# Second layer's value projection: two sets of half products with a written VectorE order in place of half products for five batches and direct matmuls for two

## The chip, the cores and the metric

The kernel runs on one core of one Trainium2 chip. The metric is the device time of one execution in microseconds (us); the time before the change is the median of three runs.

## The reference

Two layers of cross attention on x of 8 batches x 100 rows x 1024 against one context of 8 x 1444 x 512, all float32. The first layer takes a softmax over the context, the second over the query rows; the second ends in a layer norm.

```python
Q = x @ Wq + bq;  K = ctx @ Wk + bk;  V = ctx @ Wv + bv
w = softmax(Q K^T * 1024**-0.5, axis=-1)
x = x + (w @ V) @ Wo + bo                     # layer 0
q = x @ Wq + bq;  k = ctx @ Wk + bk;  v = ctx @ Wv + bv
w = softmax(q k^T * 1024**-0.5, axis=1)       # layer 1: over the rows
x = x + w @ v
out = (x - mean) * rsqrt(var + 1e-6) * gamma + beta
```

## The kernel before, in words

Keys and values are never made. `weight_products` folds Wq with Wk and Wv with Wo, `queries` multiplies x by the folded matrix, and `scores` multiplies the result by the context (transposed, `cT`, 4 units of 128 features). The weighted context A = ctx^T w (512 x 100 for a batch) is made first by `weighted_rows` (48 matmuls, line 513), and only then multiplied by the value matrix. x is held transposed in `xT` (8 blocks of 128 features x 800 columns, 100 for each batch), and the value projections add into it (`add_to_queries`, line 608).

**The loop of the second layer** (lines 864 to 887) takes the batches in turn. In `alternated` one matmul of batch b's A is followed by one score matmul of batch b + 2 (44 of them for the 48 of A); in batch 5 (`doubled`) it is followed by two, so that batch 7's scores are done halfway. Batches 6 and 7 have no scores ahead. When scores are complete, ScalarE copies them out of four PSUM banks (line 554), and `softmax1` (line 643) makes weights of them: 16 transposes of 32 x 384 on VectorE (line 589), then for each of three groups of rows a maximum (line 656), four exponentials on ScalarE (line 658), a reciprocal and a scaling on VectorE (lines 661, 662), and at last seven operations on GpSimd that sum the weights of a batch (`weight_sums`). `weight_totals` (line 682) transposes these sums of two batches on TensorE; they multiply the value bias later.

**The value projection of the second layer** is done in three sets. Batches 0 to 4 (columns 0 to 499) go after batch 5, in `project1_halves` (line 700): a 2 x 2 block product with seven half products in place of eight (`seven_products`, line 172), each of 8 matmuls of width 250, with sums of blocks on VectorE for the right side (`right_sums`) and on GpSimd, ahead of time, for the left (`project1_sums`). The right sums overwrite blocks of A1T and so have to follow products that read them. Batches 5 and 6 go after batch 6, in `project1` (line 712), as 32 plain matmuls of width 200. Batch 7 goes last, in `project_last` (line 777).

**The finish** of a batch (line 770): 8 transposes of its `xT` columns on TensorE (line 741), two passes on VectorE that add the bias term (line 745), two of statistics (line 751), and `normalise`: a power on GpSimd (line 759), a pass on VectorE (line 760), a scaling on ScalarE (line 762), an addition of beta on GpSimd (line 763) and the output DMA from GpSimd's queue (line 764). Batches 0, 1, 2 are finished under batch 6's A, 3 and 4 in whole blocks around the projection of 5 and 6, and 5 and 6 under batch 7's A. Batch 7's own finish closes the kernel: `untransposed`, `project_last`, and two output DMAs from SP and ScalarE.

**What sets the order.** TensorE runs in the order in which the program is written (`manual_schedule`, line 64). The other engines' order is made by a planner before the run, from its own costs, with earlier program text first among what it takes as ready; once made, it is fixed. Each engine then waits on semaphores at run time. PSUM has a pool of six banks (`bank`) and one of two (`bank2`); a bank is taken again once its readers are done. The inputs' loads are on SP's queue, into ten units of which gamma, beta and the value bias keep two in the second layer. `AT`, `gT`, `wT` and `row` are SBUF buffers with 2, 3, 3 and 3 slots.

Of the kernel before, what the change touches and what calls it, by code (L numbers as in the profile page):

```python
# [14 lines left out]

# [2 lines left out]

# [6 lines left out]
F32 = mybir.dt.float32  # L25
AF = mybir.ActivationFunctionType
ALU = mybir.AluOpType
# [17 lines left out]
PT = 4  # L45
G = 4
GT = G * T
G1 = 5
SCALE = 1.0 / math.sqrt(E)
EPS = 1e-6  # L50

# [2 lines left out]
def two_layer_cross_attention(ctx: ExitStack, tc: tile.TileContext, a: dict, out: bass.AP):  # L54
# [11 lines left out]
    def bank(name):  # L66
        return psum.tile([P, 512], F32, tag="ps", name=name)
# [5 lines left out]
        return stream.tile([P, E + L], F32, tag="unit", name=name)  # L73

    def wide(name):
        t = work.tile([P, LC * G1 * T], F32, tag="AT", name=name, bufs=2)
        return t[:, : LC * GT].rearrange("p (c t) -> p c t", c=LC)

    def row(name):
        return work.tile([P, E], F32, tag="row", name=name, bufs=3)  # L80

    def weight_rows(name):
        return work.tile([P, MC * T + QD * (-(-T // QD)) - T], F32, tag="wT", name=name, bufs=3)


    ones = const.tile([P, P], F32, tag="ones", name="ones")
# [60 lines left out]
                    skip_group_check=True,  # L147
                )

    def combine(to, x, y, op, engine=nc.vector):  # L150
        for t, p, q in zip(to, x, y):
            engine.tensor_tensor(t, p, q, op)

# [1 line left out]

        return [t[:, i, :] for i in range(n)]

    def left_sums(A, S, some=(0, 1, 2, 3), engine=nc.vector):
        A11, A12, A21, A22 = A
        todo = ((S[0], A21, A22, ALU.add), (S[1], S[0], A11, ALU.subtract))  # L160
        todo += ((S[2], A11, A21, ALU.subtract), (S[3], A12, S[1], ALU.subtract))
        for n in some:
            combine(*todo[n], engine)
# [7 lines left out]

    def seven_products(name, A, Bs, S, T_, nb, width, put, add, left=None, right=None):

        left, right = left or (lambda n: None), right or (lambda n: None)
        A11, A12, A21, A22 = A
        B11, B21, B12, B22 = Bs

        def pair(n, bank=bank):
            return [bank(f"{name}_{n}{j}") for j in range(2)]

        def product(banks, lhs, rhs, fresh):
            half_product(banks, lhs, rhs, fresh, nb, width)

        X = pair("x")
        product(X, A11, B11, True)
        put(0, 0, X)
        yield  # L190
        Z = pair("z")
        product(Z, A12, B21, True)
        yield
        left(0)
        right(0)
        left(1)
        right(1)
        add(0, 0, Z)
        Y = pair("y")
        product(Y, S[0], T_[0], True)  # L200
        put(1, 1, Y)
        yield
        right(3)
        product(X, S[1], T_[1], False)
        put(0, 1, X)
        yield
        left(2)
        right(2)
        W = pair("w", bank2)
        product(W, A22, T_[3], True)  # L210
        yield
        left(3)
        product(X, S[2], T_[2], False)
        add(1, 1, X)
        put(1, 0, X)
        add(1, 0, W)
        yield
        product(Y, S[3], B22, False)
        add(0, 1, Y)
        yield  # L220


    def weight_products(name, left, right, l_width, r_width, scaled):
# [32 lines left out]

        A11, A12, A21, A22 = lefts(0, 0), lefts(1, 0), lefts(0, 1), lefts(1, 1)
        B11, B12, B21, B22 = rights(0, 0), rights(0, 1), rights(1, 0), rights(1, 1)
        extra = [work.tile([P, LC * G1 * T], F32, tag="AT", name=f"{name}_s{n}", bufs=2) for n in range(2)]
        S1 = [extra[i // 2][:, i % 2 * 768 : i % 2 * 768 + lh] for i in range(H)]  # L260
        T1 = [extra[i // 2][:, i % 2 * 768 + lh : (i % 2 + 1) * 768] for i in range(H)]

# [236 lines left out]
    def shown(c):  # L499

        return MR + (MX if c >= MC - GM else 0)
# [28 lines left out]
    def scores(s, layer, cT, softmax, alone=False):  # L530
# [29 lines left out]
            )  # L560
        w = s["rows"] = weight_rows(f"w{layer}_{b}")
        s["w"] = w[:, : MC * T].rearrange("p (c t) -> p c t", t=T)
        softmax(s, parts)
        yield

    def softmax0(s, parts):
# [9 lines left out]
        rtotal = small.tile([T, 1], F32, tag="rtotal", name=f"rtotal_{b}")  # L576
        nc.vector.reciprocal(rtotal, total)
        nc.scalar.activation(p, p, AF.Copy, scale=rtotal)
        transposed(s, 0 if b else PT)

    def transposed(s, m0):

        p, w = prob[s["b"] % len(prob)], s["rows"]
        for q in range(-(-T // QD) - 1, -1, -1):
            for r in range(P // QD):
                nc.vector.transpose(  # L589
                    blocks(w, r, m0 * T + q * QD, T, MC - m0),  # L590
                    blocks(p, q, m0 * MR + r * QD, MR, MC - m0),
                )

    def blocks(t, quad, first, step, n):

# [12 lines left out]
    def add_to_queries(blocks, t0, width, banks):  # L608
        n = len(blocks) // len(banks)
        for j, ps in enumerate(banks):  # L610
            to = xT[:, blocks[j * n] : blocks[j * n] + n, t0 : t0 + width]
            nc.vector.tensor_tensor(to, to, ps[:, : n * width].rearrange("p (n t) -> p n t", n=n), ALU.add)  # L612

    def value_sums(w):

# [26 lines left out]

    def softmax1(s, parts):

        transposed(s, 0)
        for m in range(0, MC, GM):
            softmax_rows(s, m)
        weight_sums(s)

    def softmax_rows(s, m0):  # L650
        b, w, r = s["b"], s["w"], shown(m0)
        grp = slice(m0, m0 + GM)
        negmax, total, rtotal = (
            small.tile([P, GM], F32, tag=n, name=f"{n}_{b}_{m0}") for n in ("negmax1", "total1", "rtotal1")
        )
        nc.vector.tensor_reduce(negmax[:r], w[:r, grp, :], AX.X, ALU.max, negate=True)  # L656
        for m in range(GM):
            nc.scalar.activation(  # L658
                w[:r, m0 + m, :], w[:r, m0 + m, :], AF.Exp, bias=negmax[:r, m : m + 1], accum_out=total[:r, m : m + 1]
            )  # L660
        nc.vector.reciprocal(rtotal[:r], total[:r])
        nc.vector.tensor_tensor(  # L662
            w[:r, grp, :], w[:r, grp, :], rtotal[:r].unsqueeze(2).to_broadcast([r, GM, T]), ALU.mult
        )

    def weight_sums(s):

# [29 lines left out]
        left_sums(A, S, engine=nc.gpsimd)  # L697
        return A, S

    def project1_halves(A, S, At):  # L700

        n = G1 * T // 2
        Bs = [[At[:, 2 * k + i, g * n : (g + 1) * n] for i in range(2)] for g in range(2) for k in range(2)]
        t1 = work.tile([P, LC, GT], F32, tag="gT", name="o1_t1", bufs=3).rearrange("p c t -> p (c t)")
        T_ = ([t1[:, i * n : (i + 1) * n] for i in range(2)], Bs[0], Bs[2], Bs[1])

        def add(r, g, banks):
            add_to_queries([4 * r + i for i in range(4)], g * n, n, banks)

        run(seven_products("o1", A, Bs, S, T_, 4, n, add, add, right=lambda k: right_sums(Bs, T_, (k,))))  # L710

    def project1(b0, n, A, between):

        t0, t1 = b0 * T, (b0 + n) * T
        for e in range(EC):
            ps = bank(f"o1_{b0}_{e}")
            for k in range(LC):
                nc.tensor.matmul(
                    ps[:, : n * T], wv1[:, k, e * P : (e + 1) * P], A[:, k, : n * T], start=(k == 0), stop=(k == LC - 1)
                )  # L720
            to = xT[:, e, t0:t1]
            nc.vector.tensor_tensor(to, to, ps[:, : n * T], ALU.add)
            if e == EC // 2 - 1:
                between()

    def untransposed(s):

# [25 lines left out]
    def normalise(s):  # L753
# [7 lines left out]
        if b < B - 1:  # L761
            nc.scalar.activation(z, z, AF.Copy, scale=rstd)  # L762
            nc.gpsimd.tensor_tensor(z, z, beta[:T], ALU.add)  # L763
            nc.gpsimd.dma_start(out=out[b], in_=z)
            return
        for half, queue in ((slice(0, E // 2), nc.sync), (slice(E // 2, E), nc.scalar)):
            nc.vector.scalar_tensor_tensor(z[:, half], z[:, half], rstd, beta[:T, half], ALU.mult, ALU.add)
# [34 lines left out]

        return scores(batches[b], layer, *loaded(load_features(b)), softmax, alone=True)

    def alternated(b, layer, softmax, dst, doubled=False):

        nxt = b + 2 < B  # L810
        c, *cT = loaded(load_rows(b), *([load_features(b + 2)] if nxt else []))
# [1 line left out]
        ahead = scores(batches[b + 2], layer, *cT, softmax) if nxt else iter(())  # L813
        for _ in range(MC * LC):
            next(A)
            for _ in range(2 if doubled else 1):
                next(ahead, None)
            yield

    key_bias = [c0, None]  # L820
# [36 lines left out]
    run(first_scores(0, 1, softmax1))  # L857
    run(steps)
    run(first_scores(1, 1, softmax1))
    A1 = {}  # L860

    finished = {(B - 2, 0): 0, (B - 2, 14): 1, (B - 2, 28): 2, (B - 1, 6): G1, (B - 1, 22): G1 + 1}
    finishing = []
    for b in range(B):
        if b in (0, G1, B - 1):
            n = {0: G1, G1: 2, B - 1: 1}[b]
            t = work.tile([P, LC * G1 * T], F32, tag="AT", name=f"A1T_{b}", bufs=2)
            t = t[:, : LC * n * T].rearrange("p (c t) -> p c t", c=LC)
            for i in range(n):
                A1[b + i] = (t, t[:, :, i * T : (i + 1) * T])  # L870
        for n, _ in enumerate(alternated(b, 1, softmax1, A1[b][1], b + 3 == B)):
            if b % 2 and n == 8:
                weight_totals(batches[b - 1 : b + 1])
            if (b, n) in finished:
                finishing.append(finish(batches[finished[b, n]]))
            finishing = [f for f in finishing if next(f, finishing) is not finishing]
        if b == B - 1:
            run(untransposed(batches[b]))
        if b == 1:
            AS = project1_sums(wv1)  # L880
        if b == G1:
            project1_halves(*AS, A1[0][0])
        if b == B - 2:
            run(finish(batches[G1 - 2]))
            project1(G1, 2, A1[G1][0], lambda: run(finish(batches[G1 - 1])))
        if b == B - 1:
            project_last(batches[b], A1[b][0])


# [22 lines left out]
```

## Time and profile before

| what | before |
|---|---|
| median of 3 runs | 642.13 us (642.03 to 642.55) |
| the profiled execution | 642.46 us, of which the span from first to last instruction is 640.7 |
| outside the span | 1.76 us |
| granted TensorE clock, mean | 0.996 |
| TensorE matmuls busy | 631.4 us (99%) |
| VectorE, ScalarE, GpSimd busy | 450.0 (70%), 132.2 (21%), 101.7 us (16%) |
| second layer's loop begins (first A matmul) | 444.09 us |
| batch 5 under A, first projection, batch 6 under A | 542.86 to 562.98, to 586.62, to 599.42 |
| block of batch 3, second projection, batch 7 under A | 599.42 to 600.49, to 612.29, to 624.61 |
| last matmuls end, last output issued | 632.5, 637 us |

A line of the timeline gives start and duration in us, the engine, the line of the code, the operation, what it writes and reads by the program's names, the shapes and how many such instructions were merged; idle time ahead of it and what ended it stand in brackets. `128*128 128x250` is a matmul with a stationary operand of 128 x 128 and 250 moving columns. Each float32 matmul stands as two instructions, a transpose of z as one. Durations of neighbouring matmuls overlap, so their pace is read from starts.

### The profile page before, as it was taken

The page shows a single profiled execution, that of the slowest core. Times are in us where ns is not written, and L with a number is a line of the kernel's source. Part 1 is how long each engine was busy: PE and PEld are TensorE (multiplying, and loading weights), DVE is VectorE, ACT ScalarE, POOL GpSimd, SP SyncE. Part 2 cuts the span into 40 slices and gives each one's busy share as a digit, 9 for nine tenths or more (in the row PEclk, how much of TensorE's full clock was granted, in tenths as well). Part 3 has the DMA queues.
Part 4 walks back from the last instruction along what each step waited for, and adds up shares of the span by engine and source line. Part 5 has one row for each costly group of instructions (what it writes and reads, how often), then busy time and mean ns, then how long its engine had stood idle before and what let it go on. Part 6 is the DMA issues. An engine that isn't in the chain of part 4 may idle for free.

```text
span 640.7 us, 9823 instructions
## 1 busy us (share of the span) xinstructions
PE 631.4 (99%) x3920; PEld 518.4 (81%) x3920; DVE 450.0 (70%) x848; ACT 132.2 (21%) x337; POOL 101.7 (16%) x121
## 2 busy tenths in 40 slices
PE   9999999999999999999999999999999999999994
PEld 8886445568885999999998655556999999999992
DVE  5999959669723775566655798238777655896994
ACT  1010010100203333212330000123433244330221
POOL 5000000009200000000010000007211222112773
PEclk9999999999999999999999999999999999999998
DMA  8928018000089788988996203055889998940122
GB/s 292 383 101 316 0 56 333 0 1 0 2 288 367 263 310 295 329 311 311 310 315 237 97 1 131 1 176 202 284 298 315 313 307 317 303 172 1 52 78 77
DMA packets 47961, 127.28 MB, mean 199 GB/s; under 512 B 3944, under 2 KB 6504, under 8 KB 47916
## 3 DMA queue, kind: packets, MB, share of 16 engines
q1 hardware_dynamic: 45454, 119.63, 53.8%
q0 software_dynamic: 2064, 6.56, 3.2%
q8 instruction: 31, 0.51, 0.3%
q10 hardware_dynamic: 398, 0.47, 0.2%
q14 instruction: 14, 0.11, 0.1%
HBM read 123.36 MB, written 3.28 MB: 198 GB/s over the span
## 4 chain that ended last, share of the span: by engine, by line
PE 84%; issue 5%; POOL 5%; DVE 4%; ACT 2%; POOLq 0%; DVEq 0%; ACTq 0%
PE s L542 23%; PE A L513 20%; PE qk_x L141 7%; PE g_x L141 5%; PE qk_y L141 4%; PE g_y L141 3%; PE vo_x L141 3%; DVE w L589 3%; PE o_x L141 3%; POOL z L763 2%; PE qk_w L141 2%; PE vo_y L141 2%; PE qk_z L141 2%; PE g_w L141 2%; PE g_z L141 2%
## 5 line engine op out<-in xcount | busy, mean ns | idle before, releaser
L513 PE MATMUL A<-w,c 120*128 120x100 f32 (+1 forms) x1536 | 245.9, 265 | 0.0
L513 PEld LDWEIGHTS A<-w,c 120*128 120x128 f32 (+1 forms) x1536 | 215.5, 190 | 0.8
L589 DVE STREAM_TRANSPOSE w<-prob 32x384 f32<-32x384 f32 (+1 forms) x256 | 143.7, 561 | 46.4 <-ACT prob L554 15.8
L542 PE MATMUL s<-cT,g0T 128*100 128x131 f32 (+2 forms) x592 | 122.7, 296 | 0.0
L542 PE MATMUL s<-cT,g1T 128*100 128x131 f32 (+2 forms) x592 | 119.3, 296 | 0.0
L542 PEld LDWEIGHTS s<-cT,g0T 128*100 128x100 f32 x592 | 78.3, 167 | 8.3
L542 PEld LDWEIGHTS s<-cT,g1T 128*100 128x100 f32 x592 | 77.5, 167 | 8.9 <-ACT g1T L418 0.9
L554 ACT ACTIVATE prob<-s,c 100x393 f32<-100x393 f32 (+2 forms) x64 | 35.1, 560 | 116.9 <-PE s L542 116.6
L658 ACT ACTIVATE w<-w,negmax 120x100 f32<-120x100 f32 (+1 forms) x96 | 34.8, 364 | 75.1 <-DVE negmax L656 75.1
L469 POOL TENSOR_SCALAR xT<-xT,L_xattn_bo 128x800 f32<-128x800 f32 x8 | 20.8, 2607 | 133.1 <-PE qk_x L141 133.1
L571 DVE TENSOR_REDUCE maxima<-prob 100x1 f32<-100x394 f32 (+3 forms) x32 | 16.6, 528 | 28.1 <-ACT prob L554 27.9
L141 PE MATMUL qk_x<-qk 128*128 128x256 f32 x128 | 29.8, 393 | 0.0
L141 PEld LDWEIGHTS qk_x<-qk 128*128 128x128 f32 x128 | 24.7, 197 | 4.1 <-ACT qk L278 0.4
L850 POOL DMA_DIRECT2D vectors<-in_L_xattn_gamma x1 | 0.6, 602 | 163.2 <-DMA c<-in_ctx 163.2
L675 POOL TENSOR_TENSOR part<-w 120x500 f32<-120x500 f32 x8 | 10.0, 1248 | 103.5 <-PE s L542 47.3
L302 DVE SCALAR_TENSOR_TENSOR qk_L_xattn_bk<-qk,L_xattn_bk,qk_L_xattn_bk 128x1024 f32<-128x1024 f32 x14 | 17.9, 1276 | 4.0 <-DMA qk<-in_L_xattn_WqT 3.9
L612 DVE TENSOR_TENSOR xT<-xT,o_x 128x400 f32<-128x400 f32 (+1 forms) x24 | 13.5, 600 | 7.9 <-PE o_x L141 7.8
L418 ACT ACTIVATE g1T<-g_x,k 128x400 f32<-128x400 f32 x6 | 3.6, 594 | 74.2 <-PE g_x L141 63.8
L658 ACT ACTIVATION_READ_ACCUMULATOR w<-w,negmax 120x1 f32 (+1 forms) x96 | 17.9, 187 | 0.0
L763 POOL TENSOR_TENSOR z<-z,vectors 100x1024 f32<-100x1024 f32 x7 | 16.5, 2356 | 8.3 <-ACT z L762 8.3
L762 ACT ACTIVATE z<-z,rstd 100x1024 f32<-100x1024 f32 x7 | 8.0, 1149 | 39.7 <-POOL rstd L759 39.6
L662 DVE TENSOR_TENSOR w<-w,rtotal 120x400 f32<-120x400 f32 (+1 forms) x24 | 15.2, 633 | 0.5
(216 smaller groups left out, 871.8 us busy)
## 6 DMA issues: line engine op xcount, KB each, us to landing
cT<-in_ctxT SPq DMA_DIRECT2D x64, 722.0 KB, 6.7
c<-in_ctx SPq DMA_DIRECT2D x48, 768.0 KB, 7.5
c<-in_ctx SPq DMA_DIRECT2D x16, 512.0 KB, 6.6
vo<-in_L_xattn_Wo SPq DMA_DIRECT2D x8, 512.0 KB, 7.2
qk<-in_L_xattn_WqT SPq DMA_DIRECT2D x8, 512.0 KB
qk<-in_L_xattn_WqT SPq DMA_DIRECT2D x15, 256.0 KB, 5.4
qk<-in_L_xattn_WkT SPq DMA_DIRECT2D x15, 256.0 KB, 6.2
c<-in_ctx SPq DMA_DIRECT2D x16, 224.0 KB, 6.4
```

The costliest lines, as they stand in the source:

```text
L141: nc.tensor.matmul(banks[n // per][:, n % per * width : (n % per + 1) * width], lhs[i][:, n * P : (n + 1) * P], rhs[i], start=(fresh and i ...
L302: nc.vector.scalar_tensor_tensor(acc, src, cols[v][:, h : h + 1], acc, ALU.mult, ALU.add)
L469: nc.gpsimd.tensor_scalar(xT[:, e, :], xT[:, e, :], out_bias[:, e : e + 1], None, ALU.add)
L513: nc.tensor.matmul(ps[:, k * T : (k + 1) * T], c[m // CQ][:r, m % CQ, k * P : (k + 1) * P], w[:r, m, :], start=(m == 0 and k == 0), stop=( ...
L542: nc.tensor.matmul(banks[n // per][:T, cuts[n] - o : cuts[n + 1] - o], q[:, k, t0 : t0 + T], cT[k][:, cuts[n] : cuts[n + 1]], start=(k == ...
L554: nc.scalar.activation(p[:, part], ps[:T, : part.stop - part.start], AF.Identity, bias=key_bias[layer][:T, b : b + 1], scale=SCALE,)
L571: nc.vector.tensor_reduce(maxima[:, n : n + 1], p[:, part], AX.X, ALU.max)
L589: nc.vector.transpose(blocks(w, r, m0 * T + q * QD, T, MC - m0), blocks(p, q, m0 * MR + r * QD, MR, MC - m0),)
L612: nc.vector.tensor_tensor(to, to, ps[:, : n * width].rearrange("p (n t) -> p n t", n=n), ALU.add)
L658: nc.scalar.activation(w[:r, m0 + m, :], w[:r, m0 + m, :], AF.Exp, bias=negmax[:r, m : m + 1], accum_out=total[:r, m : m + 1])
L662: nc.vector.tensor_tensor(w[:r, grp, :], w[:r, grp, :], rtotal[:r].unsqueeze(2).to_broadcast([r, GM, T]), ALU.mult)
L763: nc.gpsimd.tensor_tensor(z, z, beta[:T], ALU.add)
```

## The change

1. **The sets.** The loop goes over `SETS`: batches 0 to 3, 4 to 6, and 7. The first two are projected by the new `project1`, both with seven half products, right after their last batch's A: widths 200 and 150. All right sums go to buffers of their own (a `gT` slot) and are written ahead of the products; none overwrites A1T. `project1_halves` and the direct matmuls are gone, and so is `doubled`.
2. **VectorE's order.** While `vector.in_order` is set, in `project1` alone, every VectorE instruction is bound behind the one written before it.
3. **Softmax in pieces.** `softmax1` is now a generator that stops after each transpose, after the maxima and exponentials of all three groups, and after each group's scaling. Usually it is run to its end at once. Batch 5's is not begun until the first projection: three transposes after each of the products 2 to 5, the rest after the last. Batch 7's stops after its 16 transposes; the maxima and exponentials follow the first product of the second projection, and the scalings the fourth (one) and fifth (two). In all batches the exponentials of the three groups now stand ahead of the first scaling, and their small tiles have three slots.
4. **W's additions.** Where a half product is added (not put) into its target, the two additions of W follow W itself, one product earlier. This holds in layer 0's projection too.
5. **The finishes** move: batches 0, 1, 2 under batch 4, 3 under batch 5, and 4, 5, 6 under batch 7. The outputs of batches 4 to 6 are issued by SP.
6. `weight_totals` of the pairs before the last comes at step 27 in place of 8; the last stays at 8. The `AT` slots shrink from 2000 to 1600 columns.

```diff
+SETS = (range(0, 4), range(4, 7), range(7, 8))
+LATER = {(1, 5): 0, (1, 7): 16}
...
+        if put is add:
+            add(1, 0, W)
         yield
         left(3)
         product(X, S[2], T_[2], False)
         add(1, 1, X)
         put(1, 0, X)
-        add(1, 0, W)
+        if put is not add:
+            add(1, 0, W)
         yield
...
-        softmax(s, parts)
+        s["softmax"] = softmax(s, parts)
+        for _ in islice(s["softmax"], LATER.get((layer, b))):
+            pass
...
+    def project1(bs, A, S, At, between, room):
+
+        n, t0 = len(bs) * T // 2, bs[0] * T
         Bs = [[At[:, 2 * k + i, g * n : (g + 1) * n] for i in range(2)] for g in range(2) for k in range(2)]
+        sums = work.tile([P, LC, GT], F32, tag="gT", name=f"o1_{t0}_t", bufs=3).rearrange("p c t -> p (c t)")
+        T_ = [[sums[:, (2 * k + i) * n : (2 * k + i + 1) * n] for i in range(2)] for k in range(4)]
 
         def add(r, g, banks):
+            add_to_queries([4 * r + i for i in range(4)], t0 + g * n, n, banks)
+
+        vector.in_order = True
+        right_sums(Bs, T_)
+        for _, steps in zip_longest(seven_products(f"o1_{t0}", A, Bs, S, T_, 4, n, add, add), room, fillvalue=0):
+            for _ in range(steps):
+                next(between)
+        run(between)
+        vector.in_order = False
...
+            (nc.gpsimd if b < SETS[1][0] else nc.sync).dma_start(out=out[b], in_=z)
...
-    finished = {(B - 2, 0): 0, (B - 2, 14): 1, (B - 2, 28): 2, (B - 1, 6): G1, (B - 1, 22): G1 + 1}
+    finished = {(4, 2): 0, (4, 16): 1, (4, 30): 2, (5, 34): 3, (7, 2): 4, (7, 15): 5, (7, 28): 6}
...
+            between, room = {3: (batches[5], (0, 3, 3, 3, 3)), 6: (batches[7], (1, 0, 0, 1, 2))}[b]
+            project1(bs, *AS, t, between["softmax"], room)
+    run(untransposed(batches[B - 1]))
+    project_last(batches[B - 1], t)
```

## The prediction

> **What bounds the kernel now.** I read the page first, then TensorE's waits, then TensorE's timeline around each second-layer projection, then VectorE, ScalarE and GpSimd in the same windows. The first two parts of the page:
>
> ```profile
> PE 631.4 (99%) x3920; PEld 518.4 (81%) x3920; DVE 450.0 (70%) x848; ACT 132.2 (21%) x337; POOL 101.7 (16%) x121
> ...
> PE   9999999999999999999999999999999999999994
> ...
> DVE  5999959669723775566655798238777655896994
> ```
>
> TensorE is busy in every slice but the last. Its waits hold one line, from the first microseconds:
>
> ```profile
> PE warm L90 <- DVE mhalf L105: 1.1, 1, 1.1
> ```
>
> So until 632.5 us TensorE does nothing but matmuls in its written order: a change pays by the matmul time it takes out, and costs by any wait it brings. TensorE's timeline, at the projection of batches 0 to 4 and at that of 5 and 6:
>
> ```profile
> 562.98 3.56 PE L141 MATMUL o_x<-A1T,wv 128*128 128x250 f32 x16
> 566.38 3.54 PE L141 MATMUL o_z<-A1T,wv 128*128 128x250 f32 x16
> ...
> 586.62 0.36 PE L513 MATMUL A<-w,c 120*128 120x100 f32 x2
> 586.82 0.28 PE L741 MATMUL z<-ident,xT 128*100 128x128 f32 x1
> 586.93 0.36 PE L513 MATMUL A<-w,c 120*128 120x100 f32 x2
> ...
> 599.42 1.04 PE L741 MATMUL z<-ident,xT 128*100 128x128 f32 x8
> 600.49 5.68 PE L718 MATMUL o<-A1T,wv 128*128 128x200 f32 x32
> 606.00 1.04 PE L741 MATMUL z<-ident,xT 128*100 128x128 f32 x8
> 606.88 5.58 PE L718 MATMUL o<-A1T,wv 128*128 128x200 f32 x32
> 612.29 1.70 PE L513 MATMUL A<-w,c 120*128 120x100 f32 x14
> ```
>
> Durations overlap; the starts count. Every float32 matmul is recorded as two instructions, so x16 is 8 matmuls, one half product. One product of width 250 takes 23.64 / 7 = 3.377 us (562.98 to 586.62), 0.2110 us an instruction. The second direct block takes 5.41 us for 32 instructions of width 200, 0.1691 each. The first takes 5.51, and its block of transposes 1.07 against 0.88: 0.29 us are a wait for ScalarE's copy of batch 6's A1T, and the view of that tile names it (0.3 us, once). The same timeline where batch 4 ends and batch 5 begins:
>
> ```profile
> 540.92 0.36 PE L513 MATMUL A<-w,c 120*128 120x100 f32 x2
> 541.12 0.39 PE L542 MATMUL s<-cT,g1T 128*100 128x131 f32 x2
> 541.34 0.36 PE L513 MATMUL A<-w,c 120*128 120x100 f32 x2
> ...
> 542.86 0.62 PE L542 MATMUL s<-cT,g1T 128*100 128x131 f32 x4
> 543.32 0.36 PE L513 MATMUL A<-w,c 120*128 120x100 f32 x2
> ```
>
> A pair of A and score matmul takes 0.426 us; with two score matmuls (batch 5) the step is 0.648; A alone is 0.2215 (the 14 instructions from 612.29 to 613.83 are 7 matmuls).
>
> [...] A alone, 100 wide, runs at 110.8 an instruction[...]. [...] `z<-z,mv,vectors` (line 760) takes 1.27 us alone and up to 3.35 beside GpSimd's addition of 2.36.
>
> **The change, part by part** (against the profiled execution: 642.46 us, span 640.7).
>
> 1. Projections. Out: 23.64 + 5.41 + 5.41 = 34.46 us. In: 7 products of 16 instructions of width 200, 112 x 0.1691 = 18.94; and 112 of width 150. That width is not in the trace. [...] above by the width 200 row, 18.9. The line through 200 and 250 (0.838 ns a column) gives 0.1273, the scores at 131 (0.1134) lie on it: 14.26, with 14.2 to 14.5 as ends. Sum 33.20: **-1.26**. The copy's wait goes as well: the new first products read only columns written by earlier batches (as o_x started at 562.98, before the copy at 563.18): **-0.29**.
>
> 2. Batch 5 at single rate. Out: 542.86 to 562.98 = 20.12, less 0.22 for two transposes of weight sums, 19.90. In: 44 x 0.426 + 4 x 0.2215 = 19.63: **-0.27**.
>
> 3. The 64 transposes of z move. Now 40 lie between A matmuls at 0.31 - 0.2215 = 0.09, and 24 in blocks at 0.11: 6.24 us. After: 24 in batch 4 and 8 in batch 5 lie between A and score matmuls, a mix not shown: from 0.09 to 0.11 each, I take 0.105; 24 stay at 0.09, 8 at 0.11: 6.40. **+0.16** (ends -0.3 and +0.3).
>
> 4. VectorE's fixed order. Prices: addition from PSUM 0.595 per 500 columns back to back (four in 2.43), so 0.49 for 400 and 0.39 for 300; a sum of 250 columns 0.33, so 0.28 and 0.23; a transpose 0.593. In the first projection it does 8 sums, 12 transposes and 16 additions: 2.2 + 7.1 + 7.8 = 17.2 us in 18.94. From 0.75 (A1T's copy) it runs: sums to 3.0, X to 4.0, three transposes, Z to 6.7, Y 8.3 to 9.2, three, X 11.0 to 12.0, three, W 13.8 to 14.8, three, four additions 16.5 to 18.5. TensorE needs X read by 8.1 (4.0) and by 13.5 (12.0), and X's banks for batch 6's scores from 19.1 (18.5): no wait, least slack 0.6. The second has 2.04 us a product. Batch 7's 16 transposes (9.5 us) start behind its scores, ahead of batch 6's 10.63 us of A, and end at about 10.8 even behind finish 3; the sums wait for the copy at 11.4 anyway. From the projection's start: sums to 2.6, X to 3.3, three maxima to 4.8, Z 5.6, Y 7.1, X 9.1, group 0 scaled 9.7, W 11.1, groups 1 and 2 12.3. ScalarE's twelve exponentials (0.365 each) run from 3.9 to 8.4. Weights are wanted at 14.3. Slack 2: **0**; if the cover is gone, one for one.
>
> 5. Batch 7's weight sums now start at 12.3 on GpSimd and take 4.1 us (575.75 to 579.87), to 16.5. TensorE's two transposes at step 8 come at 14.3 + 9 x 0.2215 + 6 x 0.09 = 16.8. Before, GpSimd was 30 us early. Slack 0.3, bounds 0 and 1: I take **+0.1**. Behind them on TensorE stands all of batch 7.
>
> 6. Finishes. 0 to 3 go under batches 4 and 5, where VectorE has 22 and 20 us: after 20 us of the projection it still owes batch 5 four transposes, maxima and scaling (5.6), and three finishes at 4.2 (two 0.69, two 0.65, 0.3, 1.2): 18.2. Batch 5: 13.2 for batch 6's weights and 4.2. Batch 7 gets three instead of two; batch 6 now has just that in 12.78 us, with its A1T copy held by ScalarE's scaling (line 762, 598.90 to 600.05), which is the 0.29 above. The same may come back before `ol`, behind 0.88 us of transposes: 0 to 0.9, **+0.15**.
>
> 7. Queues. Outputs 4 to 6 go from GpSimd to SP. SP issues nothing between its last load (563.6) and the end (636.3), so nothing stands behind; GpSimd saves 0.9 each, off the path: 0. Loads of batches 6 and 7 wait for slots that batch 5's quarters free, and land 7 us later, over 10 us ahead of use: 0.
>
> 8. Elsewhere. W's additions come one step earlier in layer 0's projection too, and the third maximum ahead of the first scaling. TensorE waits in neither; batch 0's first group is scaled at 443.67 for a use at 444.09. VectorE idled 0.67 us ahead of that scaling, where the maximum fits: 0, or 0.1 late.
>
> Sum: -1.26 - 0.29 - 0.27 + 0.16 + 0.1 + 0.15 = **-1.41**, 641.05 on the profiled execution. The median of the runs is 0.33 below it, so 640.7.
>
> **Rivals.**
> *A wait takes the gain back.* If VectorE's order puts batch 0's z behind all of batch 5's softmax, z_0 leaves its bank at 28.7 us after the projection's start (28.0 for the last scaling, 0.7 for one pass), and z_1, at step 16 of batch 4 (18.9 + 6.8 + 0.9 = 26.6), waits 2.1. Six banks, four with scores, speak for it; 3.3 us of waiting for exponentials, in which z_0 fits, against it. 642.13 - 1.41 + 2.1 = 642.8.
> *The last batch is VectorE's (the slower side).* In batch 7 VectorE idled 2.46 + 1.17 us ahead of the last additions. A third finish adds 4.2, less 2.1 of batch 4's remains that lay there, plus 0.8 of the projection's last additions, less 0.7 of longer cover: 1.4 are left. If line 760 meets GpSimd's addition three times, at 3.35 instead of 1.27, that is 6.2, or 5.7 more than the 0.5 of now: the end moves 4.3. 642.13 - 1.41 + 4.3 = 645.0. It decides from 1.4 us of collisions, and makes the kernel measurably slower from 4.1. For it: the 2.04 and 3.35 in the trace. Against: batch 6 with three finishes kept its pace.
> *The narrow products are no cheaper.* [...] 112 of them cost 15.6 and the gain is 0.1: 642.0. The score row at 131 speaks against it.
>
> **Chances.** Forecast 58%, with its own range 639.9 to 641.5 (width 150 and transposes near their ends, the two returns at 0 or together 0.9). First rival 22%, second 14%, third 6%. About 0.2%, 1.3 us, can be told from no change, and the forecast lies just beyond it: 48 of its 58 are faster, 10 same. The first rival gives 2 faster, 14 same, 6 slower; the second 14 slower; the third 6 same. Faster 0.50, same 0.30, slower 0.20. The range reaches from 639.8 over the first rival with some of the second, to 643.6, leaving out about 13 above and 4 below.
>
> **What would show it.** Seven o_ products of 2.71 us and seven of 2.04; batch 5 in 19.6 + 0.22 + 0.8; an A-score-transpose step of 0.53; no gap at the weight sums or ahead of `ol`; TensorE's waits still one line. Wrong if TensorE's waits name VectorE (z, xT) or GpSimd (wsum), if line 760 shows several durations over 3 us in batch 7, or if the last additions start over 0.3 us behind the last matmuls.

## The result and the profile after

| | before | after |
|---|---|---|
| median, 22 runs each | 642.47 us (641.83 to 643.35) | 641.44 us (640.59 to 642.41) |
| ratio, 95% interval | | 0.9985 (0.9979 to 0.9992) |
| profiled execution, its span | 642.46, 640.7 us | 642.15, 640.3 us |
| second layer: first A matmul to the last output's issue | 444.09 to 636.99 = 192.90 us | 444.96 to 636.23 = 191.27 us |
| last output's issue to end of span | 3.71 us | 4.05 us |

The change makes the kernel 1.03 us faster, 0.51 to 1.35 by the interval. The spans of the two profiles differ by 0.4 us only, because the profiled execution of after reached the second layer 0.87 us late. That is chance: the profiles of the twelve kernels of the experiments, which share nearly all code up to there, have their first A matmul at 443.6 to 444.25, and the median span of the 22 executions of after is 639.45 us, 0.8 less than that of the profiled one. Times inside the second layer are therefore taken from the first A matmul on. There the trace shows **-1.63 us**, and **+0.34** behind the last issue, together -1.29.

The medians of the spans, 640.7 and 639.45 us, fall by about as much. Those of the whole time fall by 1.03, because a part of the gain is lost outside the span. What an execution takes beyond the span from first to last instruction is 2.00 us in the mean of the 22 executions of after (1.79 to 2.12), and 1.78 in the mean of the 29 executions of before that were timed beside the experiments (1.72 to 1.91). Those 0.2 us stand in no trace, no step of the forecast names them, and their cause stays open; the kernels of the experiments lie between 1.78 and 2.14.

The page of after, the rows that answer to those shown of before:

```profile
PE 628.8 (98%) x3968; PEld 518.0 (81%) x3968; DVE 457.0 (71%) x864; ACT 132.1 (21%) x337; POOL 101.8 (16%) x118
...
PE   8999999999999999999999999999999999999994
...
DVE  5999959569823775666655798229786659898886
```

TensorE has 48 more instructions and is 2.6 us less busy: narrower matmuls take the place of wider ones. VectorE is fuller over the last five slices together (their digits sum to 39 in place of 37), with the work spread more evenly. TensorE's waits in after (engine and line, what released it, us in total, times, longest):

```profile
PE warm L105 <- DVE mhalf L120: 1.1, 1, 1.1
PE qk_y L156 <- DVE qk_s L93: 1.0, 1, 1.0
PE qk_x L156 <- DMA qk<-in_L_xattn_WkT: 1.0, 1, 1.0
```

The two new lines belong to the first 21 us of the kernel, where it waits for its first loads, and there the late start of this execution lies: the third product of the kernel begins at 20.87 in place of 20.00. The second layer has no wait at all. TensorE's timeline, the two projections:

```profile
523.88 2.90 PE L156 MATMUL o_x<-A1T,wv 128*128 128x200 f32 x16
...
542.85 0.36 PE L531 MATMUL A<-w,c 120*128 120x100 f32 x2
...
596.54 2.23 PE L156 MATMUL o_x<-A1T,wv 128*128 128x150 f32 x16
...
610.85 0.81 PE L531 MATMUL A<-w,c 120*128 120x100 f32 x6
```

By the starts the sets take 18.97 and 14.31 us, 33.28 together in place of 34.46. The narrow instruction costs 14.31 / 112 = 0.1278 us. One step of batch 5 with a transpose, and the last projection (`ol`):

```profile
583.03 0.36 PE L531 MATMUL A<-w,c 120*128 120x100 f32 x2
583.23 0.39 PE L560 MATMUL s<-cT,g1T 128*100 128x132 f32 x2
583.45 0.27 PE L759 MATMUL z<-ident,xT 128*100 128x128 f32 x1
583.56 0.36 PE L531 MATMUL A<-w,c 120*128 120x100 f32 x2
...
624.74 7.05 PE L803 MATMUL ol<-wv,A1T 128*100 128x512 f32 x24
```

The step takes 0.53 us: A and score 0.426, the transpose 0.109 in the mean of the eight. `ol` has no brackets, so no wait. GpSimd's last addition for batch 7's weight sums ended at 612.92, 0.44 ahead of their transposes on TensorE (613.36).

### The profile page after: what moved, and what is told of

It reads as the page before. It is cut to its first block, busy times and chain, and to the rows that moved or that the text cites. A ratio compares the mean times of both kernels' runs of the same rounds, so it can differ in the third digit from the quotient of the medians.

```text
span 640.3 us, 9944 instructions
## 1 busy us (share of the span) xinstructions
PE 628.8 (98%) x3968; PEld 518.0 (81%) x3968; DVE 457.0 (71%) x864; ACT 132.1 (21%) x337; POOL 101.8 (16%) x118
## 4 chain that ended last, share of the span: by engine, by line
PE 94%; DVE 2%; issue 1%; DMA 1%; POOL 1%; POOLq 0%; SPq 0%; ACT 0%; DVEq 0%
PE s L560 25%; PE A L531 24%; PE qk_x L156 5%; PE g_x L156 5%; PE o_x L156 5%; PE qk_y L156 4%; PE g_y L156 3%; PE vo_x L156 3%; PE o_y L156 3%; PE qk_w L156 2%; PE vo_y L156 2%; PE g_w L156 2%; PE g_z L156 2%; PE o_w L156 2%; PE o_z L156 2%; PE qk_z L156 1%
## 5 line engine op out<-in xcount | busy, mean ns | idle before, releaser
L560 PE MATMUL s<-cT,g1T 128*100 128x131 f32 (+2 forms) x592 | 122.8, 297 | 0.0
L93 DVE TENSOR_TENSOR xT<-xT,o_x 128x400 f32<-128x400 f32 (+1 forms) x32 | 15.9, 540 | 3.9 <-PE o_x L156 3.7
L759 PE MATMUL z<-ident,xT 128*100 128x128 f32 x64 | 16.3, 273 | 0.0
L93 DVE TENSOR_TENSOR w<-w,rtotal 120x400 f32<-120x400 f32 (+1 forms) x24 | 15.6, 649 | 0.7
```

The costliest lines, as they stand in the source:

```text
L93: ins = getattr(nc.vector, op)(*args, **kw)
L560: nc.tensor.matmul(banks[n // per][:T, cuts[n] - o : cuts[n + 1] - o], q[:, k, t0 : t0 + T], cT[k][:, cuts[n] : cuts[n + 1]], start=(k == ...
L759: nc.tensor.transpose(ps[:T, e * P : (e + 1) * P], xT[:, 4 * j + e, b * T : (b + 1) * T], ident)
```

## The experiments

The trace leaves four questions: whether the gain has the causes that the sum names, whether the written order and the split softmax are what keeps TensorE from waiting, how near the waits are, and where the 0.34 us at the end come from. "A to issue" below is the stretch from the first A matmul to the last output's issue (before 192.90, after 191.27), "end" what follows to the end of the span (3.71 and 4.05).

### Does the gain lie in the half products? The second set as plain matmuls

```diff
+            if b == 3:
                 project1(bs, *AS, t, between["softmax"], room)
+            else:
+                project1_direct(bs, t, between["softmax"], (1, 0, 0, 1, 1, 1, 0, 0))
```

`project1_direct` makes each of the 8 blocks of `xT` with 4 matmuls of width 300.

> The kernel after, with batches 4 to 6 projected by 64 direct matmuls of width 300 in place of 56 half products' matmuls of width 150 times two (112 instructions of 150). Theory (the gain of the set is its seven products in place of eight[...]): 64 instructions of 300 take 64 x 0.2526 = 16.17 us in place of 14.31, from first A to last issue 193.1, the time +1.9. Rival (the half products' narrower matmuls give back what they save): the same time within 0.3.

Measured: 643.86 us, ratio to before 1.0022 (1.0012 to 1.0032); A to issue 193.97. TensorE's timeline:

```profile
596.57 16.43 PE L751 MATMUL o<-A1T,wv 128*128 128x300 f32 x64 [0.58 <-ACT A1T L542]
```

Up to the next A matmul (612.83) the set takes 16.26 us (16.17 expected; 64 x 0.2529 = 16.19 by the line through the widths 200 and 250 of before) in place of 14.31: seven narrow products for eight pay 1.95 us here. In the brackets stands a wait that was not expected: the first plain matmul reads all columns, batch 6's too, and stands idle 0.58 us until ScalarE has copied them. The first half products read only batches 4 and 5's columns. So the removal of the copy's wait, a small term of the sum, is a property of the block product.

### Batch 5 with two score matmuls behind each A again

```diff
-            next(ahead, None)
+            for _ in range(2 if (layer, b) == (1, B - 3) else 1):
+                next(ahead, None)
```

> The kernel after, with two score matmuls behind each A of batch 5 again. Theory (the trace of both kernels): batch 5 goes back to 20.1 from 19.65 us, and its 8 transposes of z lie among A alone at 0.09 in place of 0.109 each: from first A to last issue 191.27 + 0.45 - 0.15 = 191.6. The prediction's own term (0.27): 191.27 + 0.27 - 0.15 = 191.4. If the mix costs nothing and the difference of the two traces had another cause: 191.1 (191.27 - 0.15).

Measured: 642.65 us, ratio 1.0004 (0.9996 to 1.0012); A to issue 192.57, 1.30 more than after. The batch itself behaves as the theory says: 564.28 to 585.33 = 21.05 us against 20.74 in after, +0.31. Most of the other 0.98 is a wait that no theory had: from the second product's start to the third's pass 2.94 us in place of 2.04. TensorE's timeline, then ScalarE's, VectorE's and GpSimd's:

```profile
598.10 2.20 PE L156 MATMUL o_z<-A1T,wv 128*128 128x150 f32 x16
601.04 2.28 PE L156 MATMUL o_y<-o_t,wv_s 128*128 128x150 f32 x16 [0.74 <-DVE o_t L93]
```

```profile
597.15 1.15 ACT L780 ACTIVATE z<-z,rstd 100x1024 f32<-100x1024 f32 x1 [11.15 <-POOL rstd L777]
```

```profile
598.72 2.41 DVE L93 TENSOR_TENSOR o_t<-A1T 128x150 f32<-128x150 f32 x2 [2.02 <-ACT A1T L542]
```

```profile
598.38 2.35 POOL L781 TENSOR_TENSOR z<-z,vectors 100x1024 f32<-100x1024 f32 x1 [1.26 <-ACT z L780]
```

With the double rate batch 7's scores are complete earlier, so its 16 transposes (9.46 us, at once, from 582.58) now stand ahead of batch 3's finish on VectorE. The finish's scaling on ScalarE begins 1.1 us behind the projection's start (in after 7.5 ahead of it), and batch 6's copy of A1T follows it at 598.21 and holds the right sums that the third product reads. By these times the late copy alone would have cost nothing, though no run has it alone: the first sum began at 598.72, and at its usual 0.30 us it would have ended 1.1 us ahead of 600.14, when the third product was due. But GpSimd's addition of batch 3's finish now lay beside it (598.38 to 600.73), and this one sum took 2.18 us, to 600.90. The single rate pays in matmul time, as forecast, and besides keeps batch 3's finish clear of the projection's copy and sums.

### The single rate alone, in the kernel before

```diff
-        for n, _ in enumerate(alternated(b, 1, softmax1, A1[b][1], b + 3 == B)):
+        for n, _ in enumerate(alternated(b, 1, softmax1, A1[b][1])):
```

> The kernel before, with batch 5 at single rate alone. Trace theory: batch 5 under A goes from 20.32 us to 19.87 (-0.45), but batch 7's sixteen transposes (9.5 us) now fall wholly into the projection of width 250, ahead of X's additions and of the second right sum in VectorE's order; TensorE then waits 2 to 3 us ahead of its fourth product, and the sum is +1.5 to +2.5 us against before. Rival (single rate pays by itself): no wait, -0.45 us.

Measured: 648.19 us, ratio 1.0084 (1.0070 to 1.0098); A to issue 198.80, +5.90. TensorE's waits, VectorE's timeline, and busy us in stretches of 2 us (TensorE, its weight loads, VectorE, ScalarE, GpSimd, then the granted clock, the DMA's busy share and its GB/s):

```profile
PE o_w L141 <- DVE A1T L152: 2.5, 1, 2.5
PE o_x L141 <- DVE A1T L152: 1.7, 1, 1.7
```

```profile
562.47 9.45 DVE L589 STREAM_TRANSPOSE w<-prob 32x384 f32<-32x384 f32 x16 [4.09 <-POOL wsum L680]
...
579.42 1.59 DVE L152 TENSOR_TENSOR A1T<-A1T 128x250 f32<-128x250 f32 x2
```

```profile
580.00:582.00 2.00, 1.33 (x4) 1.16 (x5) 2.00 (x4) 0.00 (x0) 1.88 (x4) 0.79 0.00 0
582.00:584.00 2.00, 2.00 (x6) 1.63 (x5) 0.19 (x1) 0.00 (x0) 1.18 (x3) 0.50 0.00 0
```

Two waits of together 4.2 us come from VectorE. All of batch 7's transposes lie ahead of X's first addition, as they did before; but the scores are complete later, so they begin at 562.47 in place of 559.38, and the additions and right sums behind them are late. The sum that the second wait is for takes 1.20 us in place of 0.39, beside an addition of GpSimd's weight sums (579.09 to 580.34). The rest of the loss is the clock. From 0.5 us after the wait it is granted at half (0.50 in the stretch from 582 to 584), and the product that starts at 580.67 needs 5.17 us to the next start in place of 3.37. So a part of the change that takes 0.45 us out of the matmuls costs 5.9 us in the old frame. What of the new frame it needs, the softmax in pieces or the right sums written ahead into buffers of their own, this run does not part.

### The order and the pieces of the softmax

The written order taken away from after:

```diff
-        vector.in_order = True
```

> The changed kernel with VectorE's order left to the planner, nothing else. Theory (TensorE sets the time, VectorE has slack either way): TensorE's two projections stay at 18.97 and 14.31 us, 0 us against the changed kernel, within 0.3. Rival (the written order is what keeps TensorE fed): over 1 us of waits ahead of the third to sixth products, slower than the changed kernel by as much.

Measured: 641.03 us, ratio 0.9978 (0.9968 to 0.9987); A to issue 191.26, no wait. The planner's own order is as good; the binding earns nothing measurable here. The pieces of the softmax still stand in the program between the products, so this run tests the binding and not the pieces. No run begins batch 5's softmax all at once in the new frame: that it has to be in pieces is not shown.

All of batch 7's softmax begun where its scores end, as for most batches:

```diff
-LATER = {(1, 5): 0, (1, 7): 16}
+LATER = {(1, 5): 0}
...
-6: (batches[7], (1, 0, 0, 1, 2))
+6: (batches[7], ())
```

> The changed kernel with batch 7's maxima, exponentials and scalings right behind its transposes, ahead of the right sums. Theory: VectorE stands until the last exponential (about 602 us), the right sums follow, and TensorE waits 2.6 us ahead of the second projection's third product: +2.6 us against the changed kernel (2.2 to 3.2). Rival (VectorE has slack for it): 0.

Measured: 645.96 us, ratio 1.0053 (1.0041 to 1.0066); A to issue 195.49, +4.22 against after. The first of TensorE's two new waits (the other, 1.3 us, is for additions into `xT`), and one of VectorE's right sums:

```profile
PE o_y L156 <- DVE o_t L93: 2.4, 1, 2.4
```

```profile
601.99 1.67 DVE L93 TENSOR_TENSOR o_t<-A1T,o_t 128x150 f32<-128x150 f32 x2
```

The sums start 6.2 us behind the first product (601.54; in after 0.7), since VectorE stands between the scalings and waits for ScalarE's exponentials. Two pairs of them last 1.67 and 0.94 us in place of 0.53: GpSimd now sums weights from 601.78, just beside them. The delay was foreseen, its size was not; that the sums lie beside GpSimd's work adds to it (the sums take 1.7 us more than in after, and the loss is 1.6 above the forecast). The times of the two engines go together: the sum that began at 601.99 ended at 603.37, just behind GpSimd's addition (601.78 to 603.20), as the slow one in the run with two score matmuls ended at 600.90 behind the addition that ended at 600.73. What makes them go together, no run here shows.

Four transposes of batch 5 behind each product in place of three:

```diff
-3: (batches[5], (0, 3, 3, 3, 3))
+3: (batches[5], (0, 4, 4, 4, 4))
```

> The changed kernel with four transposes in place of three in each gap of the first projection, which measures its slack. Theory: X's last additions end 1.6 us later, at 543.8 on the changed kernel's clock, and batch 6's first score matmul waits for its bank 0.2 to 0.8 us: +0.4 us. Rival (banks are taken from elsewhere): no wait, 0.

Measured: 641.14 us, ratio 0.9981 (0.9974 to 0.9988); A to issue 191.27, no wait. The 0.6 us of slack that the forecast worked out is too small: a further transpose (0.59) in each gap would have used it up. X's last additions did come later as expected (they end at 542.67, in after's time 543.98 in place of 542.31), but batch 6's first score matmul had run at 541.74, ahead of them. So these scores do not wait for X's banks; the forecast took it that they do.

The two small parts of the change (W's additions early, exponentials of all groups ahead of the first scaling), alone in the kernel before:

> The kernel before with two small parts of the change: W's additions one product earlier, and all maxima and exponentials ahead of the first scaling, with three small buffers. Theory: 0 us within 0.2, TensorE's waits one line. Rival (part of the result comes from these): over 0.3 us either way. It is also one more look at when the second layer's first A matmul starts (444.09 before, 444.96 after in the two profiles): by theory chance of the input's landing, 444.0 to 445.2.

Measured: 642.27 us, ratio 0.9999 (0.9990 to 1.0007); A to issue 192.91. They cost and bring nothing by themselves.

### Where the finishes lie

Batches 0 to 2 finished under batch 6, as in the kernel before, with all else as in after:

```diff
-    finished = {(4, 2): 0, (4, 16): 1, (4, 30): 2, (5, 34): 3, ...
+    finished = {(6, 0): 0, (6, 14): 1, (6, 28): 2, (5, 34): 3, ...
```

> The changed kernel with finishes 0, 1 and 2 back under batch 6. Theory: the 24 transposes cost 0.09 instead of 0.109 us (-0.45), but VectorE has batch 7's transposes and three finishes ahead of the right sums, so TensorE waits 7 to 9 us ahead of the second projection's third product: +6.5 to +9 us against the changed kernel. Rival (the finishes could stay): -0.45 us.

Measured: 650.76 us, ratio 1.0126 (1.0113 to 1.0140); A to issue 200.99, +9.72 against after. TensorE's timeline, and the stretches around it (columns as above):

```profile
606.79 4.34 PE L156 MATMUL o_y<-o_t,wv_s 128*128 128x150 f32 x16 [7.59 <-DVE o_t L93]
610.92 2.62 PE L156 MATMUL o_x<-o_t,wv_s 128*128 128x150 f32 x16
```

```profile
600.00:602.00 2.00, 0.00 (x0) 0.00 (x0) 2.00 (x5) 0.02 (x1) 1.90 (x1) 0.88 0.00 0
...
608.00:610.00 2.00, 2.00 (x10) 2.00 (x10) 2.00 (x6) 0.00 (x0) 2.00 (x1) 0.50 0.00 0
610.00:612.00 2.00, 2.00 (x11) 2.00 (x11) 1.91 (x5) 1.02 (x1) 1.50 (x3) 0.56 0.04 8
```

The wait is 7.6 us, and the two products after it take 4.13 and 2.45 us in place of 2.05, another 2.5 us: the granted clock is at half from 601.50, 2.3 us after the wait began, to 611.75, 5.0 us after it ended. In the single-rate kernel it is at half from 581.16, 0.5 us after the end of a wait of 2.5 us, to 584.58. In the kernel with the softmax at once a wait of about that length (2.4 us) was not followed by half the clock: its mean over the whole span is 0.996, as in after. So what a wait of about 2.5 us does to the clock can't be told from its length in these runs, and what decides it is not shown.

Five stretches between two changes of the granted clock have a common measure: 10.24 us in this kernel, 3.41 and 58.03 in the single-rate kernel, 628.05 in before (7.16 to 635.21) and 631.47 in after (4.19 to 635.66) are 3, 1, 17, 184 and 185 times 3.4133 us. Why they are, these traces do not show.

The three finishes under batch 7 begun earlier:

```diff
-(7, 2): 4, (7, 15): 5, (7, 28): 6}
+(7, 0): 4, (7, 8): 5, (7, 16): 6}
```

> The kernel after, with the three finishes under batch 7 begun at steps 0, 8 and 16 of its A in place of 2, 15 and 28. Batch 6's output is then issued over 2 us earlier. Theory A (batch 6's output lies beside the last outputs and holds their landing): from the last issue to the end of the span 3.6 to 3.9 us in place of 4.07, so the time falls by 0.1 to 0.4. Theory B (0.36 us are chance, or lie in the output's queue and not in its time): 4.0 to 4.1 as in the kernel after. From first A to last issue both expect 191.27, up to 0.3 more if z_6's passes now stand ahead of work that the end waits for.

Measured: 642.01 us, ratio 0.9997 (0.9988 to 1.0005): all of the gain is gone. A to issue is 192.00, +0.73, and the end is 4.26, not shorter but longer. TensorE's timeline and ScalarE's:

```profile
624.00 7.13 PE L803 MATMUL ol<-wv,A1T 128*100 128x512 f32 x24 [0.48 <-ACT A1T L542]
```

```profile
622.42 1.15 ACT L780 ACTIVATE z<-z,rstd 100x1024 f32<-100x1024 f32 x1 [3.96 <-POOL rstd L777]
623.48 0.47 ACT L542 COPY A1T<-A 128x400 f32<-128x400 f32 x1
```

ScalarE's scaling of batch 5 now stands ahead of the copy that `ol` reads, the very return of the copy's wait that the forecast put at 0 to 0.9. In after the copy stands first, by the planner's order:

```profile
624.07 0.49 ACT L542 COPY A1T<-A 128x400 f32<-128x400 f32 x1 [4.85 <-PE A L531]
624.46 1.15 ACT L780 ACTIVATE z<-z,rstd 100x1024 f32<-100x1024 f32 x1
```

It was near all the same: the power that this scaling needs had ended on GpSimd at 623.82, 0.25 us before the copy began.

### The 0.34 us at the end

Theory A: batch 6's output, now issued at 633.15 by SP in place of 629.28 by GpSimd, lies beside the last one and holds it. The first trial left that output out, so that its part of the result is not made:

```diff
-            (nc.gpsimd if b < SETS[1][0] else nc.sync).dma_start(out=out[b], in_=z)
+            if b != 6:
+                (nc.gpsimd if b < SETS[1][0] else nc.sync).dma_start(out=out[b], in_=z)
```

> The changed kernel with the output DMA of batch 6 left out (0.4 MB less is written, that part of the output is not made). Theory A (batch 6's late output lies beside the last output and holds its landing): from the last issue to the end 3.7 us as before, against 4.07 in the changed kernel, so -0.3 us. Theory B (the 0.34 us is chance from one execution to the next): no change in the medians beyond 0.1 us.

Measured: 641.03 us, ratio 0.9981 (0.9971 to 0.9991); the end is 3.61. That is what theory A says, and it was first taken as its proof. The second trial gave outputs 4 to 6 back to GpSimd:

```diff
-            (nc.gpsimd if b < SETS[1][0] else nc.sync).dma_start(out=out[b], in_=z)
+            nc.gpsimd.dma_start(out=out[b], in_=z)
```

> The changed kernel with all outputs but the last issued by GpSimd. Theory (after the change GpSimd ends its third addition of beta just as the last power is wanted, 633.13 against 633.15 us): three issues of 0.64 and their waits of 0.29 push the last power back by 1.5 to 2.3 us, and the end with it: +1.9 us. Rival (GpSimd is off the path, as the prediction had it): 0.

Measured: 641.37 us, ratio 0.9980 (0.9971 to 0.9988); A to issue 191.28, the end 3.97. The expected loss did not come. GpSimd's timeline in this kernel, and in after:

```profile
632.74 0.70 POOL L777 TENSOR_TENSOR rstd<-rstd,mhalf 100x1 f32<-100x1 f32 x1
```

```profile
633.23 1.52 POOL L777 TENSOR_TENSOR rstd<-rstd,mhalf 100x1 f32<-100x1 f32 x1
```

The issue does push the last power back, but the power then takes 0.70 us in place of 1.52: it begins 0.27 us ahead of the end of VectorE's pass of 1.28 us (line 778), where in after it lies beside nearly all of that pass. Either way it ends 0.4 us behind the pass.

The kernel with the early finishes then spoke against theory A: batch 6's output lay 4.5 us ahead of the last issue in place of 3.1, and the end did not shrink. The records of SP's last instructions gave another theory, C. In the traces of before and after the transfers that SP and ScalarE issue carry eight semaphores in turn (100, 102 and 112 to 117; the last four transfers of after carry 115, 116, 117 and 100), and at the end SP waits for the eight in that same order, 100 first. Each of these waits costs 0.061 us once its semaphore is there (in after the eight begin 0.061 us apart, from 638.96 to 639.39). Three more outputs on SP move the last one to another place in that order:

| kernel | the last output's place in SP's order | it lets SP go on, us after the last issue | waits behind it | end |
|---|---|---|---|---|
| before | 6 of 8 | 2.69 | 2 | 3.71 |
| after | 1 of 8 | 2.73 | 7 | 4.05 |
| without batch 6's output | 8 of 8 | 2.72 | 0 | 3.61 |
| outputs by GpSimd | 6 of 8 | 2.96 | 2 | 3.97 |
| finishes early | 1 of 8 | 2.94 | 7 | 4.26 |

So the run that seemed to prove theory A had also moved the last output to the best place. A run to part the two: batch 4's output to GpSimd, 5 and 6 left with SP.

```diff
-            (nc.gpsimd if b < SETS[1][0] else nc.sync).dma_start(out=out[b], in_=z)
+            (nc.gpsimd if b < 5 else nc.sync).dma_start(out=out[b], in_=z)
```

> The kernel after, with batch 4's output issued by GpSimd, as the kernel before has it; outputs 5 and 6 stay with SP. Theory C (the 0.36 us of the end are checks): the outputs' semaphores go round a ring of eight, and SP's last instructions check them in a fixed order, 0.061 us each. In the kernel after the very last output holds the semaphore that stands first, seven checks follow its landing; in the kernel before two followed, in the run without batch 6's output none. Here the last output's semaphore moves by one and stands last: from last issue to the end of the span 3.60 to 3.70 in place of 4.05, though batch 6's output still lies 3 us ahead of the last one. Theory A (batch 6's output lies beside the last ones and holds them): 4.0 to 4.1 as in the kernel after. From first A to last issue both expect 191.27 (batch 4's output is queued on GpSimd behind an addition that ends 1 us before the next power): the time falls by 0.4 with C, by nothing with A.

Measured: 640.87 us, ratio 0.9979 (0.9970 to 0.9987); A to issue 191.27; the end 3.61, with the last output's semaphore at place 8, there 2.71 us after the issue. Batch 6's output lay as in after, 3.1 us ahead of the last issue. SP's waits on outputs at the end, in after and then here:

```profile
SPq L916 <- DMA out<-z: 3.0, 1, 3.0
```

```profile
SPq L916 <- DMA out<-z: 2.5, 3, 1.3
```

In after SP stands at the first of its waits until everything has landed; here it takes the early ones while the last output is under way. Theory C holds and theory A falls, for SP's outputs. What stays open is when the last semaphore comes: at 2.96 with the outputs by GpSimd, but at 2.94 with the finishes early, where SP issues them, and at 2.69 to 2.83 in the other kernels, one profile each. So those 0.27 us cannot be put down to GpSimd's outputs. This kernel is at least level with after: its median is 0.57 us lower, but the two ratios to before overlap; the 0.44 us at the end are shown by the traces.

## Why the prediction was right, step by step

The forecast was 640.7, a fall of 1.41 us; the trace shows 1.63 in A to issue less 0.34 at the end, 1.29, and the medians 1.03, since 0.2 more is lost outside the span. The mechanism was the one forecast: matmul time falls and no wait comes. That the sum came so near is in part luck: against the trace the terms were off by 0.43 us one way (steps 2, 5 and 6) and by 0.55 the other (steps 1, 3 and 7). The measured median, 641.44, is 0.74 above 640.7; nearly half of that is that the kernel before had a median of 642.47 over 22 runs, not the 642.13 of three.

| step | forecast | trace | |
|---|---|---|---|
| 1 projections | -1.26 | -1.18 | 0.1278 an instruction of width 150 (0.1273 forecast) |
| 1 the copy's wait | -0.29 | -0.29 | comes back with plain matmuls (0.58) |
| 2 batch 5 | -0.27 | -0.45 | misread: see below |
| 3 transposes of z | +0.16 | +0.29 | 0.109 each between A and score (0.105 forecast), 8 in batch 5 too |
| 4 VectorE's order | 0 | 0 | slack larger than 0.6 |
| 5 weight sums | +0.1 | 0 | ready 0.44 ahead of use |
| 6 finishes | +0.15 | 0 | the copy stands first; a wait of 0.48 when begun earlier |
| 7 queues, outputs | 0 | +0.34 | SP's closing waits |
| 8 elsewhere | 0 | 0 | alone: 192.91 against 192.90 |

**Step 1** was right. What carries it is the line through the widths 200 and 250 of before, 0.838 ns a column: it gives 0.1273 us an instruction at width 150 and 0.2529 at 300, and the traces show 0.1278 (14.31 / 112) and 0.254 (16.26 / 64, the set as plain matmuls). One of its supports was weaker than it looks: the scores at width 131 could not test the line, since it gives 0.111 there, as much as A alone takes at width 100 (0.1108).

**Step 2** took 542.86 for the beginning of batch 5. That row is a pair of score matmuls; the A matmul ahead of it began at 542.66. The old stage was therefore 20.10 us without the weight sums' transposes. The new one, 565.10 to 585.84 less 0.22 and less eight transposes at 0.109, took 19.65, as worked out (19.63).

**Step 3** came out nearly at its upper end: before 40 x 0.09 + 24 x 0.11 = 6.24, after 32 x 0.109 + 24 x 0.09 + 8 x 0.11 = 6.53.

**Step 4** was right in its result. The written order is not the reason: without it there is no wait either. What the runs show to be needed is that batch 7's softmax is in pieces (4.2 us lost without) and that the finishes have left batch 6 (9.7). The least slack, 0.6 us for X's banks, was misread: batch 6's first scores do not wait for them.

**Step 7 failed.** "SP issues nothing between its last load and the end, so nothing stands behind" is true of the queue, and the 0.9 us an output that GpSimd saves were rightly called off the path. What was overlooked is that an output moved to another queue also counts in the order in which the end is waited for.

**The rivals.** The first needed a wait for z behind batch 5's softmax; TensorE's waits show none. The second had its price right and not its reach: line 760 (778 now) does last 3.14 us at 625.98 beside GpSimd's addition, once of three times under batch 7, but `ol`'s additions had room for it: the first came right behind that pass, VectorE still idled 0.52 us ahead of the second, and the last started at 632.02, 0.2 us behind the last matmuls. The third put the 112 narrow instructions at 15.6 us, an estimate of the author's that no trace supports; it falls with 0.1278 an instruction, 14.31 us. The runs with the finishes moved and the softmax whole show how near a wait is: each of them ends level with or slower than the kernel before.

## What to carry to other kernels

Where TensorE never waits, a block product with seven products pays by its instruction count, and the forecast is a count times a pace (here 112 instructions at 0.1278 us); everything else is whether VectorE and ScalarE still deliver in time, and that is decided by what stands ahead of one short copy or sum in their order, and by what GpSimd does beside it (here one sum took 2.18 us in place of 0.30). Price the wait with the clock that follows it: in two runs here 4.2 us of waiting cost 6 and 7.6 cost 10, while 3.7 cost 4.2 where the clock held. When an experiment removes something that is also counted elsewhere, as an output is, it can agree with the wrong theory; find a second one in which the two part.

## What was not expected of the hardware

- The order of the closing waits: 0.061 us for each wait behind the one that ends last, 0.43 us in after, where seven stand behind it.
- The granted clock at half after two of TensorE's waits (2.5 and 7.6 us), for 3.4 and 5.0 us of work, and not after a third (2.4 us): one product took 5.17 in place of 3.37 us, another 4.13 in place of 2.05. Five stretches between its changes are whole multiples of 3.4133 us (1, 3, 17, 184 and 185).
- A right sum on VectorE beside an addition on GpSimd: 2.18 us in place of 0.30, ending 0.17 us behind that addition.
- GpSimd's power on 100 numbers: 0.70 us where it began 0.27 us ahead of the end of VectorE's pass, 1.52 where it lay beside nearly the whole pass.
- A transpose between an A and a score matmul costs 0.109 us, between A matmuls 0.09.
